# A selective-scan kernel: softplus as one function, another tile order for GpSimd's products with C, and an earlier first product with B

## The chip, the cores and the metric

The kernel runs on one core of a Trainium2 chip. The metric is device time in microseconds (us) of one launch. The core has five engines that work from queues of their own: TensorE (PE in the profile, with its weight loads as PEld), VectorE (DVE), ScalarE (ACT), GpSimd (POOL) and SyncE (SP, which here issues the DMAs).

## What is computed

The input is eight images of 96 channels by 64 x 64. Each passes a block of layer norm, projection, depthwise convolution, four selective scans, a gated projection, two convolutions with a channel gate, linear attention, and a quantized feed-forward layer. Most of the time goes into the scans. For each of 4 directions, 192 channels and 16 states over 4096 positions:

```python
delta = jax.nn.softplus(dts + dt_projs_b[None, :, :, None])
A = -jnp.exp(A_logs)
def step(hst, inp):
    u_i, dt_i, b_i, c_i = inp
    dA = jnp.exp(dt_i[..., None] * A)
    hst = dA * hst + (dt_i * u_i)[..., None] * b_i[:, :, None, :]
    y = jnp.einsum('bkdn,bkn->bkd', hst, c_i)
    return (hst, y)
```

## The kernel before

**Units, tiles, slots.** A unit is one image, one direction and 512 positions: 8 x 4 x 8 = 256 units, 32 to an image. A unit has six tiles (`TILES`, two groups of states g by three channel groups j), and a tile is 128 partitions (two halves of states by 64 channels) by 4 states m by 512 positions. One (tile, m) is a slot: 24 slots to a unit. The loop at the end of `tile_hybrid_kernel` writes all engines' instructions slot by slot, in program order; each engine then runs its own queue in that order, as semaphores allow.

**What a slot does.** `decays` (L1123) lets ScalarE compute exp(delta x A) for the slot after next into one of four PSUM banks `da`. VectorE runs the scan (L1195), 512 elements on 128 partitions, `hst = dA * hst + x`, where x is a row of the tile `hb`. Ahead of that, `inputs` (L998, GpSimd) has filled the whole tile `hb` of 4 x 512 with B times delta times u. Six `hb` tiles exist, so a tile's buffer comes free when the unit before has summed it. After the scan the states are multiplied with C. `BANKED` says who does it: for the first `banked[n]` slots of tile n the scan writes to the PSUM bank and VectorE multiplies (`product`, L1201), one slot later; for the others the scan writes into `hb` and GpSimd multiplies them in one instruction when the tile is done (`outputs`, L1004). Ahead of it stands ScalarE's copy of the last column, the carry into the next unit (L1207; L1202 for the slots of VectorE). Then `sums` (L1024) lets TensorE add the states up in PSUM, and `gather` copies the result out.

**Step sizes.** `step_sizes` computes delta = softplus(x) in six steps spread over slots 6 to 16: a matmul into PSUM (L963), then max(x, 0) + ln(1 + exp(-|x|)) as Abs (L971), Exp (L973) and Ln (L975) on ScalarE and a maximum-and-add on VectorE (L977); then delta times u on GpSimd (L980). It does this for 128 channels two units ahead, and in odd units also for a pair: the last 64 channels of two units together. `spread` (L992) then copies delta and delta x u to the layout of the tiles by DMA from SP; `states` (L932) loads B and C, broadcast to 64 partitions.

**The plan.** `plan` puts all these steps at slots by hand. Before the change GpSimd's order in a unit is: products with C of the last unit's sixth tile (slot 0), inputs of the third (1) and fourth tile (5), products with C of the second (8), inputs of the fifth (9), delta x u (12), inputs of the sixth (13), in odd units the pair's delta x u (16), products of the fourth (16), next unit's first (17) and second inputs (21).

**Side streams.** While the scans of one image run, Python generators bring in the work of its neighbours: `front` (norm, convolution, projections of the next image) and `back_end` (gated norm, convolutions, attention, feed-forward of the last one). Each `yield n` lets n slots pass before the next step, so that results are ready when an engine gets to their reader; `PA` is 2, a wait after a matmul. `landed` waits until a load is 11 slots old. Silu and gelu need another function table on ScalarE (`table`, L275, loads it); `quiet` holds them back to the slots of `CALM`. The lines that the prediction names in them: in `gated`, the Square (L449) and the product (L450) on one PSUM tile, and L465 after the attention matmul (L463); L247, the last step of an inverse deviation, which VectorE's products L302, L476, L597 and L653 read; L636 in `joined`. In the last stage GpSimd also adds the feed-forward's result (L680).

Of the kernel before, what the change touches and what calls it, by code (L numbers as in the profile page):

```python
# [33 lines left out]
BANKED = ((4, 0, 4, 0, 4, 2), (4, 0, 4, 0, 4, 3))  # L34
# [9 lines left out]
def kernel(ctx: ExitStack, tc: tile.TileContext, a, out):  # L44
# [204 lines left out]
    def norm(k, srcs, sq, d):  # L249
# [12 lines left out]
        yield 1  # L262
# [4 lines left out]
    CALM = (0, 1, 8, 9, 16, 17)  # L267
# [138 lines left out]
    def back_end(b, s):  # L406
# [8 lines left out]
        def gated(k, cs):  # L415
# [15 lines left out]
            for n, c in enumerate(cs):  # L431
# [8 lines left out]
                yield from landed(k.ya, k.yb, k.za, k.zb, k.bs)  # L440
                for rows, (wa, wb_), z, sq in (
# [7 lines left out]
                    nc.scalar.activation(raster(sq), windowed(ps), AF.Square)  # L449
                    nc.vector.tensor_tensor(raster(z), windowed(ps), raster(z), ALU.mult)  # L450
                    yield 1
                if after in s["done"]:
                    fetch_y(after)
                    early = n + 1
# [9 lines left out]
                yield PA  # L464
# [8 lines left out]
                rs = yield from norm(k, (r, bs), k.s1[:C], k.d1[:C])  # L473
                if after is not None:
                    fetch_base(after)
                nc.vector.tensor_tensor(k.pad[0:C, :, 1 : HW + 1], square(k.d1[:C]), square(rs), ALU.mult)  # L476
# [49 lines left out]
        def second_conv(k, cs):  # L526
# [3 lines left out]
            for n, c in enumerate(cs):  # L530
# [13 lines left out]
                yield 1  # L544
# [34 lines left out]
        def attention(k, cs):  # L579

            t, x1, bs, new = k.ya.t[:C], k.za.t[:C], k.bs.t[:C], k.r[:C]
            for n, c in enumerate(cs):
# [30 lines left out]
                yield PA  # L613
# [26 lines left out]
        def feed_forward(k, cs):  # L640

            for n, c in enumerate(cs):
# [4 lines left out]
                yield PA  # L647
# [86 lines left out]
    for b in range(out.shape[0]):  # L734
# [3 lines left out]
        for order, (pair, back) in enumerate((p, k) for p in s["pairs"] for k in range(2)):  # L738
            for i in range(NC):
# [5 lines left out]
                u.banked = BANKED[int(b == 0 or u.i % 32 >= NC)]  # L745
# [207 lines left out]
    def step_sizes(us, i):  # L953

        u, which = us[0], "ab"[len(us) - 1]
        if i == 0:
            u.ps = bank("y01" if which == "a" else "y2", "dt")
            if which == "a":
                todo = [(u.ps, slice(0, P), u)]
            else:  # L960
                todo = [(u.ps[64 * h : 64 * h + 64], slice(P, DI), w) for h, w in enumerate(us)]
            for ps, d, w in todo:
                nc.tensor.matmul(ps, dt_w.rearrange("r j d -> r (j d)")[32 * w.k : 32 * w.k + R + 1, d], w.dts, start=True, stop=True)  # L963
            u.nat = sp.tile([P, T], F32, tag="nat" + which, name="nat", bufs=1)
            if which == "a":
                u.nata = u.nat
            else:
                for w in us:
                    w.natb = u.nat
        elif i == 1:  # L970
            nc.scalar.activation(u.nat, u.ps, AF.Abs)  # L971
        elif i == 2:
            nc.scalar.activation(u.nat, u.nat, AF.Exp, scale=-1.0)  # L973
        elif i == 3:
            nc.scalar.activation(u.nat, u.nat, AF.Ln, bias=one)  # L975
        elif i == 4:
            nc.vector.scalar_tensor_tensor(u.nat, u.ps, 0.0, u.nat, ALU.max, ALU.add)  # L977
        else:
            x = u.ua if which == "a" else u.ub
            nc.gpsimd.tensor_tensor(x, u.nat, x, ALU.mult)  # L980
# [19 lines left out]
    def outputs(u, n):  # L1000

        lo = u.banked[n]
        hb = u.hb[n][:, lo:, :]
        nc.gpsimd.tensor_tensor(hb, hb, u.bc[1, TILES[n][0]][:, lo:, :], ALU.mult)  # L1004
# [52 lines left out]
    def plan(u, last, nxt, third, fourth):  # L1057
# [6 lines left out]
        if last:  # L1064
            put(0, outputs, last, 5)
            for m in range(2):
                put(m, sums, last, (3, 4), 2 + m)
            for m in range(2):
                put(3 + m, sums, last, (5,), m)
            put(3, gather, last, 0)  # L1070
            put(7, states, u, 1, 1)
            put(7, gather, last, 1)
        for n in range(6):
            to = (u, n + 2) if n < 4 else (nxt, n - 4)
            if to[0]:
                put(4 * n + 1, inputs, *to)
        if third and u.i % 2:
            put(16, step_sizes, (nxt, third), 5)
        put(8, outputs, u, 1)
        put(16, outputs, u, 3)  # L1080
        for m in range(4):
            put(13 + m, sums, u, (0, 1), m)
            if m < 2:
                put(18 + m, sums, u, (2,), m)
                put(22 + m, sums, u, (3, 4), m)
# [10 lines left out]
        if third:  # L1096
# [3 lines left out]
            for i, slot in enumerate((6, 8, 9, 10, 11, 12)):  # L1100
                put(slot, step_sizes, (third,), i)
# [201 lines left out]
```

## Time and profile before

| | |
|---|---|
| median of 3 runs | 10766.89 us (10758.35 to 10770.26) |
| profiled execution | 10764.72 us, span 10763.0 us |
| VectorE busy | 10158.1 us, 94% |
| GpSimd busy | 10118.0 us, 94% |
| TensorE busy | 8423.7 us, 78% |
| ScalarE busy | 7397.8 us, 69% |
| table loads on ScalarE | 193, 1283 ns each |

The span is the time from the first instruction to the last in the profiled execution. A group's row in the profile reads: line, engine, operation, out<-in with partitions x elements and type, count | busy us in all, mean ns of one | idle us of the engine just before them, and what ended it. A wait reads: who waited, for whom, us in all, times, the longest. In a timeline the first two numbers are start and duration in us, and in the table of stretches each engine has its busy us and the number of its instructions.

### The profile page before, as it was taken

Reading aid. Unit: us, or ns where it says so; the run is one execution under the profiler, and the core shown is the slowest. Engines: PE = TensorE matmul, PEld = TensorE weight load, DVE = VectorE, ACT = ScalarE, POOL = GpSimd, SP = SyncE. Lnnn points to the kernel's source line nnn. Section 1 sums busy time; section 2 is a strip of 40 time slices with the busy share of each in tenths; the row PEclk is TensorE's granted clock in tenths of the full one; section 3 lists DMA queues with packets and bytes.
Section 4 is the critical chain, followed back from the end, with each engine's and each line's share of the span. In section 5 each row is a group of like instructions: output and inputs, shape, how many; then the busy total and the mean of one; then the engine's idle time right before and its main releaser. Section 6 shows DMA issues by size and latency. Waiting matters only on the chain. (4 is left out here: it accounts for less than half of the span.)

```text
span 10763.0 us, 97608 instructions
## 1 busy us (share of the span) xinstructions
PE 8423.7 (78%) x23270; PEld 2274.2 (21%) x23270; DVE 10158.1 (94%) x11126; ACT 7397.8 (69%) x15154; POOL 10118.0 (94%) x2782
## 2 busy tenths in 40 slices
PE   7777668886788867888688886888768887677677
PEld 2121112221122211222122221222112221111112
DVE  3999999999999999999999999999999999999993
ACT  4666666777676776777767776677766767666674
POOL 3999999999999999999999999999999999999991
PEclk8888788987889878998789887898778987778788
DMA  6888888998889988898888988889888898888883
GB/s 148 208 205 209 200 209 214 226 226 200 215 216 227 227 193 220 216 231 219 201 218 214 237 212 202 217 220 237 198 211 218 219 235 200 202 203 210 208 214 94
DMA packets 1095381, 2253.29 MB, mean 209 GB/s; under 512 B 435993, under 2 KB 436698, under 8 KB 963731
## 3 DMA queue, kind: packets, MB, share of 16 engines
q1 hardware_dynamic: 1094803, 2247.05, 84.5%
q8 instruction: 184, 3.01, 0.1%
q14 instruction: 394, 3.23, 0.1%
HBM read 1507.14 MB, written 336.69 MB: 171 GB/s over the span
## 5 line engine op out<-in xcount | busy, mean ns | idle before, releaser
L998 POOL TENSOR_TENSOR hb<-b,du 128x2048 f32<-128x2048 f32 x1536 | 6952.6, 4546 | 6.1 <-DMA du<-ua 5.2
L1024 PE MATMUL p<-hb,halves 128*64 128x512 f32 x12288 | 3713.8, 707 | 1053.0 <-POOL hb L1004 562.6
L1123 ACT ACTIVATE da<-delta,w_a_logs 128x512 f32<-128x512 f32 x6144 | 4164.3, 689 | 541.5 <-DVE hb L1195 447.5
L1195 DVE TENSOR_TENSOR_SCAN da<-da,carry,hb 128x512 f32<-128x512 f32 x3311 | 4164.0, 1274 | 90.7 <-ACT carry L1202 37.0
L1004 POOL TENSOR_TENSOR hb<-hb,c 128x2048 f32<-128x2048 f32 (+2 forms) x768 | 2714.3, 3534 | 222.3 <-ACT carry L1207 203.0
L1195 DVE TENSOR_TENSOR_SCAN hb<-da,carry,hb 128x512 f32<-128x512 f32 x2065 | 2547.0, 1265 | 1.8
L1201 DVE TENSOR_TENSOR hb<-da,c 128x512 f32<-128x512 f32 x3784 | 2534.0, 670 | 1.8 <-DMA c<-xd 0.9
L1202 ACT COPY carry<-da 128x1 f32<-128x1 f32 x3784 | 593.8, 157 | 2054.5 <-DVE hb L1201 2045.1
L1024 PEld LDWEIGHTS p<-hb,halves 128*64 128x64 f32 x12288 | 904.8, 157 | 3697.8 <-issue 1876.0
L313 PE MATMUL conv<-f0im,taps 97*128 97x512 f32 (+1 forms) x2088 | 867.7, 655 | 37.2 <-ACT f0pre L369 32.2
L1195 DVE TENSOR_TENSOR_SCAN da<-da,hb 128x512 f32<-128x512 f32 x473 | 566.1, 1214 | 28.0 <-POOL hb L998 26.6
L963 PE MATMUL dt<-dts,dt_w 7*128 7x512 f32 (+1 forms) x1024 | 485.9, 742 | 92.3 <-ACT carry L1207 36.2
L980 POOL TENSOR_TENSOR ua<-nat,ua 128x512 f32<-128x512 f32 x256 | 329.9, 1289 | 170.9 <-DVE nat L977 161.8
L313 PEld LDWEIGHTS conv<-f0im,taps 97*128 97x128 f32 (+1 forms) x2088 | 256.4, 173 | 588.2 <-issue 508.8
L1207 ACT COPY carry<-hb 128x4 f32<-128x4 f32 (+2 forms) x768 | 149.7, 195 | 302.1 <-DVE hb L1195 293.7
L1195 DVE TENSOR_TENSOR_SCAN hb<-da,hb 128x512 f32<-128x512 f32 x295 | 346.8, 1205 | 1.7 <-ACT carry L1202 1.7
L259 PE MATMUL var<-f1e,ones_c 96*96 96x512 f32 x350 | 225.6, 731 | 121.8 <-ACT f1e L256 68.5
L253 PE MATMUL ctr<-f1e,cen_c 96*96 96x512 f32 x402 | 218.1, 649 | 86.1 <-ACT f1e L592 34.2
L977 DVE SCALAR_TENSOR_TENSOR nat<-dt,nat 128x512 f32<-128x512 f32 x384 | 258.0, 672 | 17.9 <-ACT nat L975 12.7
L975 ACT ACTIVATE nat<-nat,one 128x512 f32<-128x512 f32 x384 | 271.8, 708 | 0.1
L497 PE MATMUL cab<-f1im,cab_w 97*32 97x512 f32 x1044 | 256.0, 603 | 12.5 <-DMA f1im<-xld 7.1
L275 ACT ACT_TABLE_LOAD x193 | 247.6, 1283 | 4.1 <-PEq L1292 0.8
(430 smaller groups left out, 7586.0 us busy)
## 6 DMA issues: line engine op xcount, KB each, us to landing
b<-xd SPq DMA_DIRECT2D x1024, 512.0 KB
c<-xd SPq DMA_DIRECT2D x1024, 512.0 KB
delta<-nat SPq DMA_DIRECT2D x1536, 128.0 KB
du<-ua SPq DMA_DIRECT2D x1024, 128.0 KB
y<-yt SPq DMA_DIRECT2D x512, 256.0 KB
u<-y SPq DMA_DIRECT2D x384, 256.0 KB
ua<-u SPq DMA_DIRECT2D x256, 256.0 KB
du<-ub SPq DMA_DIRECT2D x512, 128.0 KB
```

The source lines that it names most:

```text
L313: nc.tensor.matmul(ps, taps[:, t, lo : lo + n], im[:, r0 + dy : r0 + dy + 8, dx : dx + HW], start=t == 0, stop=t == 8,)
L963: nc.tensor.matmul(ps, dt_w.rearrange("r j d -> r (j d)")[32 * w.k : 32 * w.k + R + 1, d], w.dts, start=True, stop=True)
L975: nc.scalar.activation(u.nat, u.nat, AF.Ln, bias=one)
L977: nc.vector.scalar_tensor_tensor(u.nat, u.ps, 0.0, u.nat, ALU.max, ALU.add)
L980: nc.gpsimd.tensor_tensor(x, u.nat, x, ALU.mult)
L998: nc.gpsimd.tensor_tensor(hb, u.bc[0, g], u.du[j].unsqueeze(1).to_broadcast([P, G, T]), ALU.mult)
L1004: nc.gpsimd.tensor_tensor(hb, hb, u.bc[1, TILES[n][0]][:, lo:, :], ALU.mult)
L1024: nc.tensor.matmul(ps, halves, u.hb[n][:, i, :], start=TILES[n][0] == 0 and m == 0, stop=False, skip_group_check=True)
L1123: nc.scalar.activation(da[q], u.delta[j], AF.Exp, scale=a_neg[:, u.k, j, g * G + m : g * G + m + 1])
L1195: nc.vector.tensor_tensor_scan(dd if banked else x, dd, x, 0.0 if u.start else col, ALU.mult, ALU.add)
L1201: nc.vector.tensor_tensor(x, d, c, ALU.mult)
L1202: kept.append(lambda: nc.scalar.copy(col, d[:, at : at + 1]))
```

## The change

- `BANKED` goes from (4, 0, 4, 0, 4, 2 or 3) to (0, 4, 4, 0, 4, 3 or 4): of the first tile GpSimd takes all products with C, of the second VectorE takes them. In all VectorE does 3890 of the 6144 slots' products instead of 3784. The second row now goes to one unit in four, where before it went to all units but the first eight of images 1 to 7.
- Softplus becomes one ScalarE function, with a table load ahead of it and one behind it, in one block at slot 9, for one tile or (odd units) two. The three functions and VectorE's maximum-and-add go.
- `plan` moves GpSimd's steps: inputs at slots 0, 5, 8, 11 and, for the next unit, 15 and 19; products of the first tile at 4. TensorE's sums and the copies of results move with them.
- In the side streams: the slots of `CALM`, some `yield` by one more, the product in `gated` ahead of the Square, and `landed` for z and for the base later.

```diff
-BANKED = ((4, 0, 4, 0, 4, 2), (4, 0, 4, 0, 4, 3))
+BANKED = ((0, 4, 4, 0, 4, 3), (0, 4, 4, 0, 4, 4))
...
         inv_std(ps, ps)
-        yield 1
+        yield 2
...
-    CALM = (0, 1, 8, 9, 16, 17)
+    CALM = (4, 5, 16, 17, 18, 19)
...
-                yield from landed(k.ya, k.yb, k.za, k.zb, k.bs)
+                yield from landed(k.ya, k.yb)
...
                     yield PA
-                    nc.scalar.activation(raster(sq), windowed(ps), AF.Square)
+                    yield from landed(k.za, k.zb)
                     nc.vector.tensor_tensor(raster(z), windowed(ps), raster(z), ALU.mult)
                     yield 1
+                    nc.scalar.activation(raster(sq), windowed(ps), AF.Square)
+                yield 1
...
                 nc.tensor.matmul(ps, wy[1][up], k.zb.t, start=False, stop=True)
-                yield PA
+                yield PA + 1
                 nc.vector.tensor_tensor(r, ps, r, ALU.mult)
...
-                u.banked = BANKED[int(b == 0 or u.i % 32 >= NC)]
+                u.banked = BANKED[int((b == 0 or u.i % 32 >= NC) and u.i % 4 == 0)]
...
-    def step_sizes(us, i):
...
-        elif i == 1:
-            nc.scalar.activation(u.nat, u.ps, AF.Abs)
-        elif i == 2:
-            nc.scalar.activation(u.nat, u.nat, AF.Exp, scale=-1.0)
-        elif i == 3:
-            nc.scalar.activation(u.nat, u.nat, AF.Ln, bias=one)
-        elif i == 4:
-            nc.vector.scalar_tensor_tensor(u.nat, u.ps, 0.0, u.nat, ALU.max, ALU.add)
...
+    def step_sizes():
+
+        table("softplus")
+        for us, ps in dt_sums:
+            which = "ab"[len(us) - 1]
+            nat = sp.tile([P, T], F32, tag="nat" + which, name="nat", bufs=1)
+            nc.scalar.activation(nat, ps, AF.Softplus)
...
+        table("natural_log_exp_and_others")
+        dt_sums.clear()
...
         if last:
             put(0, outputs, last, 5)
-            for m in range(2):
-                put(m, sums, last, (3, 4), 2 + m)
+            for m in range(1, 4):
+                put(m - 1, sums, last, (3, 4), m)
...
-            put(3, gather, last, 0)
+            put(5, gather, last, 0)
+            put(7, gather, last, 1)
...
-        for n in range(6):
+        put(4, outputs, u, 0)
+        for n, slot in enumerate((0, 5, 8, 11, 15, 19)):
             to = (u, n + 2) if n < 4 else (nxt, n - 4)
             if to[0]:
-                put(4 * n + 1, inputs, *to)
+                put(slot, inputs, *to)
...
-        put(8, outputs, u, 1)
         put(16, outputs, u, 3)
         for m in range(4):
-            put(13 + m, sums, u, (0, 1), m)
...
+            put(11 + m, sums, u, (0, 1), m)
...
+            put(6, step_sums, (third,))
             if u.i % 2:
-                for i, slot in enumerate((9, 11, 12, 13, 15)):
-                    put(slot, step_sizes, (nxt, third), i)
+                put(8, step_sums, (nxt, third))
+            put(9, step_sizes)
+            put(12, scaled_input, (third,))
```

## The prediction

> **What bounds the kernel now.** I read the page's busy line first, then the stretches of one image, then who waits for whom, and last the groups and a piece of timeline.
>
> ```profile
> PE 8423.7 (78%) x23270; PEld 2274.2 (21%) x23270; DVE 10158.1 (94%) x11126; ACT 7397.8 (69%) x15154; POOL 10118.0 (94%) x2782
> ```
>
> Two engines, VectorE and GpSimd, are busy for 94% of the span, so neither alone is the answer. Counting 24 scans to a unit in VectorE's timeline gives each unit's start: the scan stage runs from 181.0 to 10532.7 us, and six of the eight images (1 to 6) take 1299 to 1301 us each. Here is image 4 in quarters of eight units:
>
> ```profile
> core 0: us, PE busy (x) PEld busy (x) DVE busy (x) ACT busy (x) POOL busy (x), PEclk, DMA share, GB/s
> 5341.70:5671.80 330.10, 263.92 (x698) 70.59 (x694) 320.59 (x348) 221.68 (x467) 321.14 (x86) 0.86 0.88 219
> 5671.80:5997.70 325.90, 279.95 (x827) 70.42 (x826) 313.15 (x340) 233.01 (x456) 313.65 (x85) 0.91 0.90 221
> 5997.70:6323.40 325.70, 292.28 (x847) 85.86 (x847) 318.18 (x355) 236.97 (x487) 313.52 (x86) 0.86 0.90 227
> 6323.40:6641.00 317.60, 211.11 (x548) 53.38 (x546) 313.00 (x340) 234.15 (x489) 316.98 (x93) 0.76 0.82 199
> ```
>
> In quarter 4 GpSimd has no idle time: it is the bound there. In quarters 1 to 3 both engines lose 7 to 13 us each: they hand each other waits. These are the waits, VectorE's first (total, times, longest):
>
> ```profile
> DVE da L1195 <- POOL hb L998: 62.9, 67, 6.9
> DVE f1x L450 <- ACT f1e L449: 56.3, 33, 4.2
> DVE da L1195 <- ACT carry L1202: 37.0, 19, 3.2
> DVE f1pre L450 <- ACT f1pre L449: 34.2, 50, 2.6
> ```
>
> and GpSimd's greatest:
>
> ```profile
> POOL hb L1004 <- ACT carry L1207: 203.0, 159, 7.9
> ```
>
> In GpSimd's timeline 175 us of its waits at L1004 (126 waits) fall 8 to 16 us into a unit: that is the products with C of the second tile, which need the scans of slots 4 to 7. So GpSimd arrives there before VectorE has finished, in the same kernel in which VectorE, at the first tile, waits for GpSimd.
>
> **The change, part by part.** Durations are these, by form; what a removed or added instruction is worth is the distance of starts in the timeline, since neighbours overlap a little (a product 0.59 us, the maximum-and-add at L977 0.60, a scan 1.19, GpSimd's 512-wide product 1.22, its 1024-wide 2.32, its 2048-wide 4.49).
>
> ```profile
> L1201 DVE TENSOR_TENSOR hb<-da,c 128x512 f32<-128x512 f32 x3784 | 2534.0, 670 | 1.8 <-DMA c<-xd 0.9
> L1004 POOL TENSOR_TENSOR hb<-hb,c 128x512 f32<-128x512 f32 x200 | 258.2, 1291 | 20.4 <-ACT carry L1207 18.9 <-DMA du<-ua 0.6 <-DMA f1x<-td 0.6
> L977 DVE SCALAR_TENSOR_TENSOR nat<-dt,nat 128x512 f32<-128x512 f32 x384 | 258.0, 672 | 17.9 <-ACT nat L975 12.7 <-ACT carry L1202 4.5
> L1004 POOL TENSOR_TENSOR hb<-hb,c 128x1024 f32<-128x1024 f32 x56 | 132.3, 2362 | 4.2 <-ACT carry L1207 4.0
> ```
>
> *1, work of VectorE and GpSimd.* All 384 instructions of L977 go, 12 in a quarter: -7.2 us. The products on VectorE go from 14 to 15 a unit in each image's first quarter (images 1 to 7), +8 x 0.59 = +4.7; elsewhere one unit in four goes from 15 to 16, +2 x 0.59 = +1.2 a quarter. VectorE: -2.5 in quarter 1, -6.0 in each other. GpSimd: quarter 1 exchanges eight 1024-wide forms for 512-wide, -8.8; each other loses two 512-wide, -2.4. For image 4 VectorE then has 318.1, 307.1, 312.2 and 307.0 us of work, GpSimd 312.3, 311.2, 311.1 and 314.6; the greater of each pair sums to 1256 against 1299 now.
>
> *2, order of the tiles.* I lay a unit out by hand with the starts above and 0.05 us a slot for side work. Before: slots 4 to 7 end at 12.3, the carry is copied, and the second tile's products may start at 12.6; GpSimd gets there at 10.9, so it waits 1.7. It then comes to the next unit's first product so late that in an odd unit this ends 1.8 us before VectorE needs it. Between "GpSimd waits" and "VectorE waits" lie only 0.1 us. After: the first tile's scans end at 5.0, its products may start at 5.3, GpSimd gets there at 6.3; next unit's first product ends at 30.2, needed at 38.6; the tightest inputs now are the fourth tile (15.4, needed at 19.0) and next unit's second (40.5, needed at 43.6). The two engines may drift by about 3 us before either waits. From both sides: all of the 203 and 63 stay, or none. I take them as nearly gone, 1 us a quarter, since the hand table is nearest to this trace's own waits. Nothing else is late by this: next unit's first b has been asked for at about 9 us and is used at 25.7 (before, at 33.2); 128 KB spreads land 2 to 3 us after their issue (the ua load that waits for them shows it), and du of the third tile has 10 us instead of 15. What stands behind that spread on SP (the plain loads, b, results of the side streams) goes out some 3 us later in odd units; the side streams count 11 slots for a load, and GpSimd's DMA waits are some 33 us in all.
>
> *3, softplus block.* Abs, Exp and Ln (577, 617 and 707 ns) become one function, between two table loads. The trace has no softplus; I bound it by the cheapest and dearest of the three and take 0.6. It has such blocks for silu:
>
> ```profile
> 5011.26 0.68 ACT L1123 ACTIVATE da<-delta,w_a_logs 128x512 f32<-128x512 f32 x1
> 5011.95 1.28 ACT L275 ACT_TABLE_LOAD   x1
> 5013.25 1.48 ACT L321 ACTIVATE f0pre<-f0pre 128x1536 f32<-128x1536 f32 x1
> 5014.75 1.28 ACT L275 ACT_TABLE_LOAD   x1
> 5016.04 0.16 ACT L1202 COPY carry<-da 128x1 f32<-128x1 f32 x1
> ```
>
> Each load takes 1.28 us and the next instruction follows within 0.02. A softplus block is 1.28 + 0.6 + 1.28 = 3.2 us, 3.8 in odd units (two functions). ScalarE gets 512 x 1.28 - 384 x 1.3 = +157 us at 69%: nothing in itself. On the path: the block starts when slot 11's decay is done, at 14.2 in the table of starts (slot 9's scan starts at 13.5); then come a carry copy and slot 12's decay, done at 18.2, in odd units at 18.8. VectorE has slots 9, 10 and 11 ahead, each a scan with a product, and wants slot 12 at 19.0. It is covered by 0.2 to 0.8 us; without that cover it costs what it overruns. Read in the changed kernel's instruction order, 222 of 254 blocks have nothing more before that decay; the others carry one or two copies (0.6 to 1.2 us). From both sides: 0, and the 53 us that scans wait for ScalarE now around 87 blocks, 0.6 each, 156 in all. I take 0.1 a unit, near the hand table. The softplus itself waits for its dt matmul, the pair's now only one slot ahead; queued behind it are the second load and that decay. By the table PE has 3 us for it; ScalarE now waits 35.9 us for these matmuls in all (33 times). The silu and gelu blocks move to slots 4, 5 and 16 to 19; the same table covers them by 0.5 to 1.1 us at 4, 5 and 16, and by nothing at 18 and 19: a few tenths for some of 87.
> The Trainium skill ("ScalarE: Activation LUTs", section "What ACT_TABLE_LOAD costs") adds a drain of 1380 ns to each switch, 2.66 us in all, and from this asks for few switches. The rows above show 1.28 and no drain; by the page the block would be 5.9 to 6.5 us, the decay 2 to 2.5 us late in every unit, and the kernel slower, an estimate of 11,000.
>
> *4, order in the side streams.* L450 waited for the Square that was issued just ahead of it on the same PSUM tile; now it stands first, its matmuls are issued before z has landed, and the Square goes a slot later. There it waits for VectorE's product; behind it stand a carry copy and a decay, which wait for nearly the same place of VectorE anyway. Over images 1 to 6 this wait is 4.7 us an image in quarter 1 and 8.7 in quarter 2; I leave 1 and 2. One slot more after a variance or attention matmul takes most of L465 (2.7 an image) and of the waits for L247 (3.6). Both ends: all of it stays, or nothing. The steps' clock starts every unit at the same count as before (2 more from the prologue on), so no stream is left over to be drained.
>
> *5, start and end.* Two blocks stand ahead of the first scan; the chain dt, softplus, spread is 1.28 longer and two functions shorter: +4 at most.
>
> **The sum for image 4.** Quarter 1: 318.1 + 2.4 of waits = 320.5 (now 330.1). Quarter 2: VectorE 307.1 + 2 (L450) + 4.8 (ScalarE, 4.0 now) = 313.9, + 1 = 314.9 (325.9). Quarter 3: 312.2 + 0.5 + 0.8 (L636) + 4.1 (ScalarE) = 317.6 (325.7). Quarter 4: GpSimd 314.6 + 1 = 315.6 (317.6). That is -30.7; six such images -184. Image 0 has GpSimd as its bound throughout (idle only in its first units): 4 x -2.4 = -10. Image 7: VectorE -20.5 of work, waits about -5: -25. Start +4. Total -215: 10764.7 (the profiled execution; span 10763.0) - 215 = 10550. The median of the runs shown is 10766.9, 2 above: no correction.
>
> **The rivals.** *Only work leaves:* the waits stay, just elsewhere. Image 4: -2.5 - 6.0 - 6.0 - 2.4 + 2.4 for blocks = -14.5; six are -87, images 0 and 7 -28: 10650. For: L1207's copies, PE and the sums behind them stay on GpSimd's path, and the sums of the fourth tile now stand close behind its products. Against: the 3 us. *All waits go:* -43 x 6 - 10 - 30 = -299: 10466. *Slower, the softplus block at slot 9:* its cover is under 1 us. Waits after silu blocks recur at 3.19, 0.88 and 2.06 us, mean 2.04. At that price for every block, 168 units where VectorE is the bound pay 343, the other 88, with 0.9 us of slack, 100: -215 + 443 = 10993. It decides from 1.3 us a bound unit (215/168). *Nothing:* the block costs about those 1.3: 10765; GpSimd's gain in quarter 4 and image 0 is small anyway.
>
> **How the numbers follow.** Forecast 0.50, only work 0.20, all waits gone 0.10, nothing 0.08, slower 0.12. Faster by over 0.2% (about what can be told from no change here): the first three, 0.80. The range takes these three and the forecast with the blocks at their upper bound (156 in place of 25: 10681), with some 15 to either side: 10450 to 10695; that leaves out 0.20.
>
> **What would show it.** Right: GpSimd's wait for L1207 under 60 us; no waits of VectorE for L998 outside quarter 4 and image 0; no row of L977; 384 softplus rows near 0.6 us; table loads at 1283; L450 waiting under 20 us. Wrong: scans at slot 12 waiting for their decay by over 0.5 us a unit, a table load with a gap behind it, first products (L998 before) waiting for PE or DMA.

## The result, and the profile after

| | before | after |
|---|---|---|
| median | 10763.9 us (4 runs) | 10868.7 us (4 runs, 10858.0 to 10875.6) |
| ratio | 1 | 1.0096, 95% interval 1.0079 to 1.0114 |

The change makes the kernel some 105 us slower, where 215 less was forecast. The page's busy line of the changed kernel, to be held against the one of before:

```profile
PE 8265.9 (76%) x23270; PEld 2253.6 (21%) x23270; DVE 10079.8 (93%) x10848; ACT 7660.4 (70%) x14954; POOL 9991.0 (92%) x2732
```

VectorE and GpSimd have 78 and 127 us less to do, and the span is 111 us longer (10873.9): the time went into waits. Between its instructions from the first scan to the last, GpSimd's idle time went from 252 to 489 us and VectorE's from 270 to 456. Image 4 by quarters:

```profile
5401.25:5744.64 343.39, 282.14 (x710) 72.88 (x710) 323.34 (x352) 237.99 (x481) 316.58 (x86) 0.87 0.89 219
5744.64:6076.11 331.47, 275.54 (x848) 72.06 (x848) 318.45 (x331) 239.30 (x449) 307.07 (x84) 0.87 0.89 215
6076.11:6397.93 321.82, 260.74 (x772) 76.84 (x768) 307.79 (x338) 241.20 (x475) 312.04 (x84) 0.87 0.89 223
6397.93:6715.32 317.39, 203.72 (x583) 53.80 (x582) 307.10 (x328) 239.50 (x470) 312.77 (x89) 0.78 0.81 198
```

Only the third quarter is faster than before (321.8 against 325.7), the fourth is as it was; the first lost 13 us and the second 6. In quarters 1 and 2 the two engines idle for 13 to 27 us each. VectorE's waits of the changed kernel (scans are L1210 now, products L1216):

```profile
DVE da L1210 <- ACT da L1135: 109.2, 104, 4.3
DVE hb L1210 <- ACT carry L1217: 87.7, 124, 2.8
DVE da L1210 <- ACT carry L1217: 55.3, 36, 3.7
DVE hb L1210 <- ACT da L1135: 50.6, 66, 2.3
```

Together 303 us, all for ScalarE's decay or the carry copy ahead of it; 150 of VectorE's idle us stand before the scan of slot 12, behind the softplus block, in 184 of the 256 units. GpSimd's waits (outputs are L1014, inputs L1006):

```profile
POOL hb L1014 <- ACT carry L1222: 203.0, 70, 12.9
...
POOL hb L1006 <- issue: 144.7, 56, 7.2
POOL hb L1006 <- PE dy L447: 32.9, 6, 6.8
POOL hb L1006 <- DMA c<-xd: 22.8, 6, 5.2
POOL hb L1006 <- PE p L1034: 22.0, 6, 9.6
```

The 203.0 us for the carry copies are still there, by chance to the tenth, but most of them (168) now stand at the sixth tile, at slot 0. Six of these waits, 77 us, are the 12.90 us behind the long `dgate` shown below; where `dgate` is short, in a_gate_psum, this row is 129.7 us. The L1006 rows are new: before, GpSimd's inputs waited for 6 us in all. Now next unit's first product alone waits 242 us, in 96 units.

"issue" and the other names are what the profile takes for the last to come. What these waits have in common shows in TensorE's timeline. The product fills the buffer that TensorE's sums of the first two tiles (L1034) have to leave first, and in 79 of the 96 units, 197 us, it starts 0.13 us after the last of these sums ends. Here is one from image 4; the sums end at 5557.49:

```profile
5553.31 1.26 POOL L988 TENSOR_TENSOR ua<-nat,ua 128x512 f32<-128x512 f32 x1
5553.96 3.53 PE L1034 MATMUL p<-hb,halves 128*64 128x512 f32 x12
5557.62 4.53 POOL L1006 TENSOR_TENSOR hb<-b,du 128x2048 f32<-128x2048 f32 x1 [3.05 <-issue]
```

TensorE's own waits in front of the sums, first before, then after (`nat` is the softplus that has to leave the bank which the first sum takes):

```profile
PE p L1024 <- POOL hb L1004: 562.6, 189, 9.3
PE p L1024 <- DVE nat L977: 489.6, 142, 12.2
```

```profile
PE p L1034 <- POOL hb L1014: 988.2, 180, 16.8
PE p L1034 <- ACT nat L976: 322.1, 133, 7.4
```

All 988 us stand in front of the first sum of the fourth and fifth tiles (485 of the 563 before): GpSimd's products of the fourth tile now come behind next unit's first product.

One row was not on anybody's list. Unit 14 of images 1 to 7 went from 39.6 to some 52 us, and this instruction is in it (the tile `dgate`, 96 x 96, the identity times a gate; smallest, median and greatest duration in ns):

```profile
L577 DVE TENSOR_SCALAR dgate<-ident,gate x8: 265/13105/13243, 2058.6 to 10754.4; 96x96 f32<-96x96 f32 x8
```

Before, the same row reads

```profile
L572 DVE TENSOR_SCALAR dgate<-ident,gate x8: 266/3771/3777, 2123.4 to 10648.6; 96x96 f32<-96x96 f32 x8
```

The change doesn't touch its code. It takes 0.27 us in the tail, where GpSimd is idle. Here it is in image 4, with GpSimd's instructions beside it, first before, then after:

```profile
6021.22 4.51 POOL L998 TENSOR_TENSOR hb<-b,du 128x2048 f32<-128x2048 f32 x1
...
6022.02 3.77 DVE L572 TENSOR_SCALAR dgate<-ident,gate 96x96 f32<-96x96 f32 x1
...
6027.29 4.53 POOL L1004 TENSOR_TENSOR hb<-hb,c 128x2048 f32<-128x2048 f32 x1 [1.56 <-ACT carry L1207]
```

```profile
6009.17 4.50 POOL L1006 TENSOR_TENSOR hb<-b,du 128x2048 f32<-128x2048 f32 x1
...
6009.68 12.96 DVE L577 TENSOR_SCALAR dgate<-ident,gate 96x96 f32<-96x96 f32 x1
6013.63 4.48 POOL L1014 TENSOR_TENSOR hb<-hb,c 128x2048 f32<-128x2048 f32 x1
6018.09 4.48 POOL L1006 TENSOR_TENSOR hb<-b,du 128x2048 f32<-128x2048 f32 x1
...
6035.47 1.27 POOL L1014 TENSOR_TENSOR hb<-hb,c 128x512 f32<-128x512 f32 x1 [12.90 <-ACT carry L1222]
```

Before, it ends (6025.79) when GpSimd's running instruction ends and GpSimd pauses for 1.56 us. After, GpSimd has three instructions back to back, and VectorE's ends (6022.64) with the third of them, when GpSimd has to wait for the very scans that VectorE could not do. Images 1 to 7 all show the same, with 1.56 us of pause before and 12.9 after.

### The profile page after: what moved, and what is told of

Read it like the earlier page. It is cut to its first block, busy times and chain, and to the rows that moved or that the text cites. A ratio compares the mean times of both kernels' runs of the same rounds, so it can differ in the third digit from the quotient of the medians.

```text
span 10873.9 us, 96968 instructions
## 1 busy us (share of the span) xinstructions
PE 8265.9 (76%) x23270; PEld 2253.6 (21%) x23270; DVE 10079.8 (93%) x10848; ACT 7660.4 (70%) x14954; POOL 9991.0 (92%) x2732
## 5 line engine op out<-in xcount | busy, mean ns | idle before, releaser
L1006 POOL TENSOR_TENSOR hb<-b,du 128x2048 f32<-128x2048 f32 x1536 | 6947.3, 4545 | 248.5 <-issue 144.7
L1034 PE MATMUL p<-hb,halves 128*64 128x512 f32 x12288 | 3722.6, 720 | 1310.7 <-POOL hb L1014 988.2
L1210 DVE TENSOR_TENSOR_SCAN da<-da,carry,hb 128x512 f32<-128x512 f32 x3385 | 4277.5, 1274 | 163.2 <-ACT da L1135 97.5
L1014 POOL TENSOR_TENSOR hb<-hb,c 128x2048 f32<-128x2048 f32 (+1 forms) x718 | 2588.7, 3605 | 247.6 <-ACT carry L1222 203.0
L1216 DVE TENSOR_TENSOR hb<-da,c 128x512 f32<-128x512 f32 x3890 | 2604.0, 669 | 1.2
L1210 DVE TENSOR_TENSOR_SCAN hb<-da,carry,hb 128x512 f32<-128x512 f32 x1991 | 2442.6, 1264 | 141.9 <-ACT carry L1217 79.5
L1034 PEld LDWEIGHTS p<-hb,halves 128*64 128x64 f32 x12288 | 904.9, 161 | 3921.4 <-issue 2315.5
L275 ACT ACT_TABLE_LOAD x705 | 904.5, 1283 | 12.8 <-PEq L1307 0.8
L1210 DVE TENSOR_TENSOR_SCAN da<-da,hb 128x512 f32<-128x512 f32 x505 | 607.8, 1214 | 32.3 <-POOL hb L1006 15.1
L967 PE MATMUL dt<-dts,dt_w 7*128 7x512 f32 (+1 forms) x1024 | 441.2, 661 | 68.1 <-ACT carry L1217 35.5
L1222 ACT COPY carry<-hb 128x4 f32<-128x4 f32 (+1 forms) x718 | 139.4, 194 | 463.9 <-DVE hb L1210 454.5
L1210 DVE TENSOR_TENSOR_SCAN hb<-da,hb 128x512 f32<-128x512 f32 x263 | 304.6, 1203 | 39.5 <-POOL hb L1006 31.2
L1059 ACT COPY yt<-p 128x512 f32<-128x512 f32 x368 | 213.2, 579 | 90.5 <-PE p L1039 76.0
L976 ACT ACTIVATE nat<-dt 128x512 f32<-128x512 f32 x384 | 216.7, 596 | 16.4 <-PE dt L967 7.2
```

What stands on the lines that cost most here:

```text
L275: nc.scalar.preload_act_table_set(name)
L967: nc.tensor.matmul(to, dt_w.rearrange("r j d -> r (j d)")[32 * w.k : 32 * w.k + R + 1, d], w.dts, start=True, stop=True)
L1006: nc.gpsimd.tensor_tensor(hb, u.bc[0, g], u.du[j].unsqueeze(1).to_broadcast([P, G, T]), ALU.mult)
L1034: nc.tensor.matmul(ps, halves, u.hb[n][:, i, :], start=TILES[n][0] == 0 and m == 0, stop=False, skip_group_check=True)
L1210: nc.vector.tensor_tensor_scan(dd if banked else x, dd, x, 0.0 if u.start else col, ALU.mult, ALU.add)
L1216: nc.vector.tensor_tensor(x, d, c, ALU.mult)
```

## The experiments

**Theory 1:** the time is lost in three places: `dgate` waits until GpSimd pauses, which in the changed kernel is three instructions later instead of one; the softplus block has no cover at slot 12; and the new order only moves the waits, to next unit's first product. **Rivals:** the softplus block alone (the prediction's own slower case), or the side edits meeting the new order. All runs in one table; "order" is `BANKED`, the plan's slots and `CALM` together, and "V" and "S" say who makes `dgate`, VectorE or ScalarE:

| kernel | order | side edits | softplus | dgate | us | ratio to before, 95% |
|---|---|---|---|---|---|---|
| after | new | yes | block | V | 10868.7 | 1.0079 to 1.0114 |
| a_gate_psum | new | yes | block | V, from PSUM | 10780.7 | 1.0001 to 1.0023 |
| b_gate | old | no | three functions | S | 10741.5 | 0.9966 to 0.9986 |
| b_side | old | yes | three functions | V | 10757.9 | 0.9981 to 1.0004 |
| b_side_gate | old | yes | three functions | S | 10677.1 | 0.9900 to 0.9930 |
| b_softplus | old | no | block | V | 10772.2 | 0.9995 to 1.0017 |
| b_side_soft_gate | old | yes | block | S | 10591.2 | 0.9822 to 0.9851 |
| a_three_functions | new | yes | three functions | V | 10831.4 | 1.0044 to 1.0089 |
| b_order_gate | new | no | three functions | S | 10957.1 | 1.0154 to 1.0184 |
| a_gate_noside | new | no | block | S | 10923.4 | 1.0127 to 1.0157 |
| a_gate_noloads | new | yes | Exp, no loads | S | 10674.9 | 0.9898 to 0.9927 |
| b_side_calm_gate | old, new `CALM` | yes | three functions | S | 10729.4 | 0.9953 to 0.9979 |
| a_three_oldcalm_gate | new, old `CALM` | yes | three functions | S | 10989.6 | 1.0193 to 1.0227 |
| best_calm | old, new `CALM` | yes | block | S | 10693.6 | 0.9919 to 0.9949 |
| best_split | old, new split | yes | block | S | 10660.1 | 0.9886 to 0.9915 |
| best_early | old, early inputs | yes | block | S | 11035.6 | 1.0232 to 1.0266 |
| a_gate_late | new, late inputs | yes | block | S | 10727.5 | 0.9947 to 0.9977 |
| best_exp_ln | old | yes | Exp and Ln | S | 10552.1 | 0.9788 to 0.9820 |
| best_exp_ln_apart | old | yes | Exp and Ln apart | S | 10597.8 | 0.9833 to 0.9862 |

In the kernels of the old order with a block silu's and gelu's slots are 0, 1, 16 and 17 (in best_calm the new ones, in best_exp_ln_apart the old); in those of the new order with three functions Abs, Exp and Ln stand one slot earlier than before. So the price of the block and that of the order each hold such a move.

### dgate

```diff
+            ps = bank(k.tag, "dg")[:C, :C]
+            nc.tensor.matmul(ps, ident[:C, :C], ident[:C, :C], start=True, stop=True)
+            yield PA
-            nc.vector.tensor_scalar(dgate, ident[:C, :C], gate, None, ALU.mult)
+            nc.vector.tensor_scalar(dgate, ps, gate, None, ALU.mult)
```

> The changed kernel, with one edit: the 96x96 instruction dgate (L577) reads the identity from PSUM (a matmul copies it there first) instead of from SBUF. Theory 1 (VectorE's instruction waited for GpSimd to pause): it takes 0.3 us or less instead of 13.1, in the middle of GpSimd's train, and unit 14 of images 1 to 7 goes from 52 back to about 40 us: 10869 - 70 to - 90 = 10780 to 10800. Rival (it waited for something else, for example the table load of the silu block beside it): it still takes some 13 us and the time stays at 10869.

The changed kernel with the identity read from PSUM: `dgate` takes 0.30 us with GpSimd as busy as ever, and the time falls by 88 us, as Theory 1 said. In the kernel before, with the same job on ScalarE:

```diff
-            nc.vector.tensor_scalar(dgate, ident[:C, :C], gate, None, ALU.mult)
+            nc.scalar.activation(dgate, ident[:C, :C], AF.Copy, scale=gate)
```

> The kernel before, with one instruction per image moved: dgate = ident x gate is made by ScalarE (a copy with a scale) instead of VectorE. Theory 1 (VectorE's dgate waits until GpSimd pauses; in the kernel before 3.77 us in each of seven images, some 3.5 more than its work): 7 x 3.5 = 24 us less, a little more where the wait also upset the order: 10730 to 10745. Rival (the instruction is long for a reason of its own, or its wait is hidden by GpSimd being the bound in that unit): no change, 10755 to 10770.

25 us less than the before of the same chip, 7 x 3.5 as expected. So the wait is on the path in both kernels.

How long it lasts isn't settled by GpSimd's pauses alone. In before, after, b_side and b_softplus it ends in all seven images 0.06 to 0.07 us after the last GpSimd instruction ahead of a pause of at least 1.56 us. In a_three_functions it does so in two images (11.7 us); in the other five it lasts 2.85 us and ends with the instruction that was running, although GpSimd's next follows at once. From image 4:

```profile
5998.92 4.52 POOL L1003 TENSOR_TENSOR hb<-b,du 128x2048 f32<-128x2048 f32 x1
6000.65 2.85 DVE L577 TENSOR_SCALAR dgate<-ident,gate 96x96 f32<-96x96 f32 x1
6003.40 4.52 POOL L1011 TENSOR_TENSOR hb<-hb,c 128x2048 f32<-128x2048 f32 x1
```

Why it is let in there and passed over twice in the changed kernel, no run shows.

The Trainium skill ("SBUF — State Buffer", section "Who interferes with whom") states that VectorE and GpSimd share a port pair, that a `tensor_scalar` from SBUF can be one of the operations that need it, and that the second to issue blocks until the first has finished. That names a mechanism that fits; the runs show who waits and what ends it. By the page the wait would end with the one GpSimd instruction that was running. So it does in before and in the five images of a_three_functions; in the changed kernel that would be 4.0 us, and the trace has 12.96, through three.

### Side edits

The hunks of the change in the side streams, alone, in the kernel before:

```diff
         inv_std(ps, ps)
-        yield 1
+        yield 2
...
-                    nc.scalar.activation(raster(sq), windowed(ps), AF.Square)
+                    yield from landed(k.za, k.zb)
                     nc.vector.tensor_tensor(raster(z), windowed(ps), raster(z), ALU.mult)
                     yield 1
+                    nc.scalar.activation(raster(sq), windowed(ps), AF.Square)
```

> The kernel before, with the side streams' edits alone (product ahead of the Square, one slot more behind some matmuls and variances, later waits for z and base). Forecast theory: L450 and L247 wait less, some 12 us an image in the quarters that VectorE bounds: 10764 - 70 = 10695. Rival (VectorE only waits for TensorE in place of ScalarE, as in the changed kernel, where L450 and L467 wait 100 us): within 20 us of 10764.

10757.9: almost nothing, the rival's number. But the trace has `dgate` at 11.4 us in six images here, 7.6 more than before (10.3 in the seventh): it stands until the end of the fourth GpSimd instruction in a row. With `dgate` on ScalarE:

> The kernel before with the edits of the side streams alone (yields, the product ahead of the Square, later landed) and dgate on ScalarE. Theory 1: with dgate on VectorE the same edits made 10757.9, with a dgate of 11.4 us in seven images; without it they bring what part 4 of the prediction was after and somewhat more: 10757.9 - 7 x 11.2 = 10680, at most 10705. Rival (the edits are worth nothing, and the long dgate stood where VectorE had time): 10735 to 10760, the same as the kernel before with dgate on ScalarE.

10677.1, 64 below the same kernel without the edits. Theory 1's number, and near the 70 that the expectation of b_side took for the edits: `dgate` had hidden it. L450 waits 18 us here, 99 before.

### Softplus

```diff
-            for i, slot in enumerate((6, 8, 9, 10, 11, 12)):
-                put(slot, step_sizes, (third,), i)
...
+            put(6, step_sums, (third,))
+            if u.i % 2:
+                put(8, step_sums, (nxt, third))
+            put(9, step_sizes)
+            put(12, scaled_input, (third,))
...
-    CALM = (0, 1, 8, 9, 16, 17)
+    CALM = (0, 1, 16, 17)
```

> The kernel before, with softplus as one function in a block at slot 9 (and silu and gelu kept from slots 8 and 9), all else as before. Theory 1: VectorE loses 227 us of work, some 160 of them count, and gets waits of 150 at slot 12: about 10760, no gain. Rival (the block is cheap, the order costs): 10764 - 160 = 10605.

No gain although VectorE has 206 us less to do, as Theory 1 expected. It gave the wrong reason, though: VectorE idles 66 us at slot 12, not 150, and the same edit on top of b_side_gate does gain:

> The kernel before with the edits of the side streams, dgate on ScalarE and the softplus block at slot 9 (with the calm slots 0, 1, 16, 17, since silu's blocks at 8 and 9 would meet it). It is the changed kernel without its order of tiles and its split of the products. Without the block this is 10677.1. Theory 1 (the old order gives the block no cover: what VectorE saves on the maximum-and-add, 258 us of busy time, comes back as waits at slot 12 and of GpSimd's inputs, as it did alone, where it brought nothing): 10665 to 10695. Rival (the block is worth its saved work where the side streams no longer collide with it): 10560 to 10630.

10591.2, the rival's side: with the side edits and a short `dgate` the block is worth 86 us. Without them it was worth nothing, though VectorE idles more at slot 12 here (109 us) than there. Now GpSimd is the bound; from the first scan to the last it idles for 84 us in all. In the changed kernel the opposite edit, the three functions and the maximum-and-add put back:

```diff
-            put(9, step_sizes)
-            put(12, scaled_input, (third,))
+            for i, slot in enumerate((6, 7, 8, 9, 10, 12)):
+                put(slot, step_sizes, (third,), i)
```

> The changed kernel, with delta by Abs, Exp, Ln and VectorE's maximum-and-add again (at slots 7 to 10, in odd units the pair's at 11 to 15), all else as changed. Theory 1 (the softplus block costs most): the 150 us that scans wait at slot 12 go, the sums of the first two tiles start earlier since their PSUM bank is free earlier, VectorE gets 227 us of work back, of which some 100 count: 10869 - 150 - 50 + 100 = 10770. Rival (the order of the tiles costs most): only work comes back, 10869 + 100 = 10970.

10831.4, neither number. Slot 12's waits go (5 us left), but others of 51 and 43 us stand at slots 8 and 10 (59 and under 10 in the changed kernel), and part of the gain is that `dgate` is 2.85 us in five images here. Then the loads alone (this kernel computes Exp in place of softplus):

```diff
-        table("softplus")
-            nc.scalar.activation(nat, ps, AF.Softplus)
+            nc.scalar.activation(nat, ps, AF.Exp)
-        table("natural_log_exp_and_others")
```

> The changed kernel with dgate on ScalarE and without the two table loads of the softplus block, and with Exp in place of softplus (so the step sizes are exp(x) here, not softplus). Against 10780.7 it prices the loads. Theory 1 (the block's loads make VectorE wait 145 us at slot 12 and hold TensorE's sums, and most of that is on the path): 10640 to 10690. Rival (those waits only move elsewhere, and the order is what costs): 10740 to 10775.

106 us less than a_gate_psum, of some 655 us that the loads last (2.57 a block). VectorE's idle time at slot 12 falls from 146 to 49 us, and GpSimd's for next unit's first product from 250 to 161: TensorE waits 61 us for softplus's bank instead of 320, so the sums start sooner. The last two runs take the loads out and keep the function, in the old order:

```diff
+            nc.scalar.activation(nat, ps, AF.Exp)
+            nc.scalar.activation(nat, nat, AF.Ln, bias=one)
```

> The 10591.2 kernel (kernel before, side edits, dgate on ScalarE, softplus in a block at slot 9) with softplus as ln(1 + exp(x)), Exp and Ln from the table that the scans' decays use: no table load, one function more, and still no maximum-and-add on VectorE. It holds as long as exp(x) doesn't overflow. Theory 1 (in the old order GpSimd is nearly always busy, with some 85 us of idle time in the whole scan stage, so the loads can cost that at most): 10510 to 10580. Rival A (the loads cost as in the changed kernel, where taking them out brought 106): 10470 to 10500. Rival B (the waits at slot 12 are not on the path at all, since GpSimd is the bound): 10585 to 10600.

10552.1, 39 below the block, inside Theory 1's range: GpSimd had little idle time left to win. It is the fastest version of these runs, 2.0% below the kernel before. Its busy line:

```profile
PE 8554.1 (81%) x23270; PEld 2289.6 (22%) x23270; DVE 9907.1 (94%) x10734; ACT 7207.9 (68%) x14778; POOL 10110.6 (96%) x2782
```

GpSimd has as much work as in the kernel before, and hardly waits.

```diff
-    CALM = (0, 1, 16, 17)
+    CALM = (0, 1, 8, 9, 16, 17)
-            put(9, step_sizes)
+            put(8, step_sizes)
...
+                put(11, step_sizes)
```

> The same with the pair's two functions apart from the first tile's (slots 8 and 11 instead of one block at 9) and the kernel before's own calm slots (0, 1, 8, 9, 16, 17). Theory 1 (no block of over 1.3 us stands ahead of a decay, and silu has its six slots): the same as the other or up to 20 less. Rival (silu's blocks at 8 and 9 meet Exp and Ln there): 10 to 40 more than the other.

46 more by the medians, on the rival's side; its four runs lie apart, 10584 to 10615, so 32 to 63 more. The scans wait 149 us for their decay, 40 in the other. Which of the two edits does it was not separated.

### Order

All of the order, but without side edits, with three functions and then with the block:

```diff
-BANKED = ((4, 0, 4, 0, 4, 2), (4, 0, 4, 0, 4, 3))
+BANKED = ((0, 4, 4, 0, 4, 3), (0, 4, 4, 0, 4, 4))
-    CALM = (0, 1, 8, 9, 16, 17)
+    CALM = (4, 5, 16, 17, 18, 19)
...
+        for n, slot in enumerate((0, 5, 8, 11, 15, 19)):
```

> The new order of tiles, the new split of the products and the new calm slots alone: three functions for softplus as before, no edits in the side streams, and dgate on ScalarE. Theory 1 (the order frees GpSimd of its waits for the second tile but moves them to next unit's first products and to the sixth tile, so it brings little): 10710 to 10750, 0 to 30 below the kernel before with dgate on ScalarE. Rival A (part 2 of the prediction, the order is worth some 100 us, and only softplus's block eats it): 10620 to 10650. Rival B (the order itself costs time, some 15 us an image in each first quarter, where TensorE's sums come late): above 10770.

216 above b_gate: rival B, and far beyond its bound. GpSimd's wait for next unit's first product, 7 us in b_gate, is 416 here; in all old-order kernels but best_split (30) and best_early it is 5 to 15.

> The changed kernel without its edits in the side streams and with dgate on ScalarE: order and softplus block alone. Against the changed kernel with dgate read from PSUM (10780.7, side edits in). Theory 1 (the first quarters' +15 us an image come of the product ahead of the Square meeting the new order: matmuls issued before z has landed hold up TensorE's queue): the first quarters fall back by some 10 us in six images, the other quarters lose the 5 to 8 that the edits bring: 10760 to 10790, with quarter 1 of image 4 at 330 to 336. Rival (they come of the order or of the softplus block): quarter 1 stays at 343 to 347 and the time goes up, 10800 to 10840.

143 above a_gate_psum, worse than even the rival said. Theory 1's part on the first quarter was half right: in image 4 it falls from 344.7 to 334.7, but the second rises from 320.5 to 334.5 and the third from 321.4 to 329.2. The side edits are not what spoils the new order; they help it more than the old (143 against 64). So the order itself costs, and these runs take it apart. First `CALM`, with the side edits and three functions, in the old order and out of the new one:

> The kernel before with the edits of the side streams, dgate on ScalarE and the changed kernel's calm slots (4, 5, 16 to 19) for silu's and gelu's blocks. With the old calm slots it is 10677.1. Theory 1 (what is wrong with the new order is TensorE's sums and matmuls that stand behind one another, not the calm slots): 10665 to 10700. Rival (a block at slots 4 and 5, with a copy of results behind it, makes VectorE wait some 3 us, and at 18 and 19 it has no cover): 10730 to 10790.

> The changed kernel's order and split with its side edits, but three functions for softplus, the old calm slots (0, 1, 8, 9, 16, 17) and dgate on ScalarE: against 10677.1 this is the order and the split alone. With the new calm slots and a dgate of 11.7 us in VectorE's way it was 10831.4, some 10750 without that dgate. Theory 1 (the order itself costs the time): 10735 to 10775. Rival (the calm slots cost it and the order is worth something): 10620 to 10680.

10729.4, 52 more: the edge of the rival. The other way round 10989.6: neither, and the old slots are far worse in the new order. (The 10750 in this expectation is too low: `dgate` was long in two images only, so it should have said some 10795, an estimate.) Blocks and order have to fit each other; neither set of slots is good in itself. Then one part at a time on top of b_side_soft_gate, 10591.2:

> The kernel before with side edits, dgate on ScalarE and the softplus block (10591.2), and the changed kernel's calm slots 4, 5, 16 to 19 in place of 0, 1, 16, 17. Without the block these calm slots cost 52. Theory 1 (they cost about the same with it, and the order of tiles the other 140): 10620 to 10660. Rival (with the block the blocks of silu at 4 and 5 crowd ScalarE, and this is most of the 190 between this kernel and the changed one): 10700 to 10790.

102 more; between the two. The scans wait for ScalarE at slots 7, 8 and 19, behind silu's and gelu's blocks.

```diff
-        put(8, outputs, u, 1)
+        put(4, outputs, u, 0)
```

(with the new `BANKED`)

> The same 10591.2 kernel with the changed kernel's split alone: GpSimd multiplies the first tile at slot 4 and VectorE the second, one unit in four with all of the sixth tile on VectorE; the slots of the inputs and sums as before. Theory 1 (the split is sound, it takes 121 us off GpSimd, which is busy for 96% here, and puts some 60 on VectorE; what costs is next unit's first product ahead of the fourth tile's products): 10540 to 10610. Rival (the split is what costs: the wait at the second tile's products moves to the first tile's, whose scans are the first of the unit): 10660 to 10760.

69 more, the edge of the rival. GpSimd's waits for the carry copy go from 75.7 us to 216.1, 108 of them just ahead of the first tile's products. So the split by itself brings back the wait that it was to remove.

```diff
-                put(4 * n + 1, inputs, *to)
+                put(slot, inputs, *to)
...
-            put(13 + m, sums, u, (0, 1), m)
+            put(11 + m, sums, u, (0, 1), m)
```

> The same 10591.2 kernel with the changed kernel's slots for the inputs alone (0, 5, 8, 11, 15, 19, so next unit's first product stands ahead of the fourth tile's products with C, and the sums of the first two tiles two slots earlier, at 11 to 14); the split as before. Theory 1 (GpSimd then asks for the first tile's buffer before TensorE's sums have freed it, and has no time to wait): 10680 to 10760. Rival (earlier inputs do no harm by themselves): 10570 to 10620.

11035.6: GpSimd waits for TensorE's sums as Theory 1 said, but the cost is 444 us where it named 89 to 169. This edit does more than move next unit's first product. The fifth tile's input, at slot 8 now, comes ahead of the second tile's products, and the sums of these stand two slots earlier. TensorE waits 583 us in front of the second tile's sums (67 in b_side_soft_gate); in the changed kernel, where VectorE makes these products, it doesn't wait there at all. So the run shows such a ring of waits, but 444 is not the price of the early product in the changed kernel. GpSimd's waits of this kernel have one new row:

```profile
POOL hb L1006 <- PE p L1032: 418.7, 167, 8.7
```

and its timeline in image 4 shows how the wait goes round (matmuls `p` L1032 are the sums, `xdbl` a side stream's):

```profile
5927.28 4.50 POOL L1012 TENSOR_TENSOR hb<-hb,c 128x2048 f32<-128x2048 f32 x1
...
5931.83 1.97 PE L1032 MATMUL p<-hb,halves 128*64 128x512 f32 x2 [6.16 <-POOL hb L1012]
...
5942.93 0.58 ACT L399 COPY f0e<-xdbl 80x512 f32<-80x512 f32 x1 [9.79 <-PE xdbl L392]
...
5943.98 4.53 POOL L1006 TENSOR_TENSOR hb<-b,du 128x2048 f32<-128x2048 f32 x1 [6.50 <-PE p L1032]
5944.13 1.29 DVE L1207 TENSOR_TENSOR_SCAN da<-da,carry,hb 128x512 f32<-128x512 f32 x1 [7.16 <-ACT da L1132]
```

GpSimd finishes the second tile's products at 5931.78. TensorE has stood in front of their sums for 6.16 us, with all that is queued behind them. ScalarE in turn waits 9.79 us for one of those matmuls, with the decays queued behind that copy, and so VectorE waits 7.16 us for a decay. GpSimd itself waits 6.50 us for the sums that free the buffer which its early product is to fill. Last, next unit's two early inputs alone, taken back in the changed kernel (the sums stay two slots early):

```diff
-        for n, slot in enumerate((0, 5, 8, 11, 15, 19)):
+        for n, slot in enumerate((0, 5, 8, 11, 17, 21)):
```

> The changed kernel with dgate on ScalarE and with next unit's first and second inputs back at slots 17 and 21, so the fourth tile's products with C stand ahead of them again. Against 10780.7. Theory 1 (GpSimd's waits for next unit's first product, some 200 us at slots 15 to 19, go, and with them most of the order's cost): 10640 to 10700. Rival (the wait goes to the other steps, and the order costs by the sums or the calm slots): 10760 to 10800.

53 less, between the two: GpSimd's waits for next unit's first product go from 250 us to 12, TensorE's for GpSimd's products from 998 to 474, but GpSimd's for the carry copies rise from 130 to 280 (all against a_gate_psum); 158 of these now stand at the fourth tile's products.

## Why the prediction was wrong

Following the table's rows: b_gate -25, side edits -64, softplus block -86, the new order +190 (b_side_soft_gate to a_gate_psum), `dgate` on VectorE +88: +103. These are steps from one kernel to the next, so but for a few us by which the kernel before differs between chips they have to add up to the measured +105 and prove nothing by it; each step is a run. The parts of the order don't add up (102, 69 and 444 alone, 190 together), so what each is worth inside the changed kernel stays open, but for the early inputs: 53.

- *Step 1, work of VectorE and GpSimd: right.* Summed over all images the steps make -168 and -122; measured are -169 (a_gate_psum, without the long `dgate`) and -127. But the sum made each quarter the greater of the two engines' work and a few us of waits, and less work doesn't give less time by itself: b_softplus takes 206 us off VectorE and gains nothing.
- *Step 2, order of the tiles: the step that failed most.* "Nothing else is late by this" was wrong. The hand table held only VectorE and GpSimd. It let next unit's first product start at 25.7 us into the unit; in the trace, where GpSimd waits for the sums, it starts at 28.3 (median, up to 35.0). In the old order GpSimd came to this product after the fourth tile's products, in the new one an instruction of 4.5 us sooner, and TensorE's sums had not left its buffer: 242 us of waits, 6 before. The fourth tile's products then come later, and TensorE's queue stands in front of their sums, 988 us for GpSimd's products in all (563 before). The bank that softplus holds is not what grew: 322 us, 490 before. The 3 us by which the two engines "may drift" had no TensorE in them. The 203 us for the carry, which were to fall under 60, are 130 without the long `dgate`, and VectorE's waits for inputs are still 60 us (L1006; 63 before at L998).
- *Step 3, softplus block: its instructions right, its cover wrong.* Function 596 ns (0.6 forecast), loads 1283 with no gap behind. The cover of 0.2 to 0.8 us came from the same hand table, which had the block start at 14.2 us into a unit; in the trace it starts at 15.2 in even and 14.9 in odd units (medians). Measured are 150 us of waits at slot 12, where 25 were taken and 156 was the upper bound. Taking the loads out gives 106. That is in the new order; in the old one the block gains 86, and its loads cost 39.
- *Step 4, side edits: near in size, but the wait came back in the new order.* The step takes 62 off L450 and most of 38 off two others; in the old order the edits bring 64, in the new one 143 (a_gate_noside). But L450 still waits 62 us in the changed kernel, for its own matmul now (L447), where under 20 was forecast.
- *Step 5, start: harmless.* The first scan starts at 179.6, 1.4 us sooner.
- *What no step held:* an instruction that isn't touched can change its length; this term, 88 us, was put at nothing. The row of `dgate` was there before the change, 3.77 us against 0.27 for the same 96 x 96; its timeline shows that it ends with GpSimd's instruction, at one of the pauses for the second tile's products that the change was made to take away.
- *The signs and the rivals:* two of the prediction's signs of being wrong came, slot 12's waits at 0.59 us a unit and first products waiting for TensorE. "Slower" was right in sign and named a real cost, but for the block alone, at 443 us; its loads are worth 106. "Only work leaves" had TensorE's sums as something that stays on GpSimd's path. The case that came, waits for TensorE that grow, had no price.

## What to carry to other kernels

When two engines are both near 95% and hand each other buffers, lay out the third one too: list for each moved step which instruction frees the buffer that it writes, on which queue that one stands and what is ahead of it there. Measure edits that come together one by one, with the others in place too: two of the parts here looked worthless alone (side edits beside a long `dgate`, softplus without the side edits) and were worth 64 and 86 us. Check what else a run moves before its time is put down to one cause, as with best_early. And explain every instruction that takes much longer than its size says before making its neighbour busier.

## What the runs showed of the hardware

- A small VectorE instruction from SBUF to SBUF with a scalar per partition stood for 2.85 to 13.2 us beside a busy GpSimd and 0.27 us beside an idle one; with its operand in PSUM it took 0.30 beside a busy GpSimd, and on ScalarE 0.375. All 35 long ones (seven images of five kernels) end 0.06 to 0.07 us after a GpSimd instruction does. In 30 GpSimd then pauses; in five its next instruction follows at once. So it can be let in between two GpSimd instructions, and it can be passed over there, twice in the changed kernel.
- 705 table loads took 1283 ns each, in both directions, and the softplus function after one took 596 ns for 128 x 512, less than Exp with Ln (1.3 us) but, with its two loads, dearer. The Trainium skill ("ScalarE: Activation LUTs", section "Table sets: the hidden batching unit") says that Exp and Ln lie in one set, so that no load stands between them; best_exp_ln has 512 loads fewer than the block and is 39 us faster.
